# In one of the two depthwise pairs that need a second product, 128-row tiles give way to two rounds of 64x32 tiles, a VectorE tap, and a scan split three to one

## The chip, the cores and the metric

The kernel runs on one core of one Trainium2 chip. The metric is device microseconds from the start to the end of the program. The kernel before took 1713.65, 1717.79 and 1720.6 us in three runs (median 1717.79). One more execution was profiled; it took 1714.65 us, of which the trace spans 1712.9 us.

## The reference, cut to what matters

Four images of 128 channels and 96x96 points are group-normalised and read as sequences of 9216 points in four directions: along the rows, along the columns, and both backwards. Each of the 16 sequences goes through the same block, and the four directions are fused by a 1x1 convolution and added to the input.

```python
t = _grouped1x1(x, in_proj_w, in_proj_b, G)
u, gate = (t[:, :HID], t[:, HID:])
u = silu(u)
u = conv_general_dilated(u, dw_w, padding=[(2, 2)], feature_group_count=HID)   # depthwise, K = 5
s = conv1x1(u, ssm_in_w)
a = DMIN + (DMAX - DMIN) * sigmoid(conv1x1(u, ssm_delta_w, ssm_delta_b))
bb, cc = tanh(conv1x1(u, ssm_b_w, ssm_b_b)), tanh(conv1x1(u, ssm_c_w, ssm_c_b))
hst = exp(cumsum(log(a))) * cumsum(bb * s * exp(-cumsum(log(a))))
u = u + conv1x1(cc * hst + ssm_d * s, ssm_out_w)
u = _grouped1x1(u * sigmoid(gate), mix_w, mix_b, G)
return conv1x1(u, out_proj_w, out_proj_b)
```

The change concerns the five-tap depthwise convolution of the first 128 of the 256 hidden channels.

## The kernel before, in words

**Pairs and steps.** For each image the kernel makes a pass over columns (V) and one over rows (H); a pass treats a forward sequence and its backward partner together, as two streams s = 0 and 1. A pass has six stages of 16 lines. Within a stage the sequence is split by position modulo 4 into four phases p, each 384 points long. A *pair* is one phase of one stage for both streams; there are 192 pairs, numbered t. Four pairs make a *step* (48 steps), and k = t % 4 is the place in the step; the phases come in the order p = 1, 2, 3, 0. In the first three stages of a pass (`fresh`) the input projection is computed; in the last three the two streams meet stages that the other one has been through, and tiles are reused or read back mirrored.

**The convolution.** The hidden activations lie in a tile `sil` with 4 phases x 32 channels on 128 partitions, so that one product with a 128x32 matrix of diagonals (`band`, `conv`, L724) adds up to four taps of one phase. For p = 3 and p = 0 (`alone`, L733; k = 2 and 3) the 128-row product holds four taps, and the fifth is added by VectorE from an extra tile `lone` in `add_lone` (L768, L775), which also moves the sum from PSUM to the tile `u`. For p = 1 and p = 2 (k = 0 and 1) the taps fall three and two on either side of a block border: the 128-row product takes one side, and a 64-row product (`less`, `conv_less`, L784), of which eight tiles of 64x32 run side by side, takes the two taps of the other. ScalarE then copies the sum from PSUM banks 6 and 7 to `u` (`copy_u`, L801). The other 128 channels get their five taps from ScalarE (first tap, L826) and VectorE (L828) in PSUM banks 0 and 1.

**One pair.** All instruction streams are written in order by hand (`pair_on`, L1041). TensorE has, in each pair: the output products of the pair before the last six (`accumulate`, two of 8 matmuls, results in banks 2 or 4 and 5), the convolution, then gate or input projections and the products from the scan (`out_of`, L650, banks 0 to 3), then the projection of `u` (`proj`, 16 matmuls with the weights `main`, banks 4 and 5). In fp32 each matmul of the source is two instructions in the trace. ScalarE copies the output products out of PSUM into tiles `ys` (L946), which GpSimd adds to the accumulator `acc` (`add`, L963). VectorE multiplies by the gate (L711), runs the scan (L903: 64 partitions, two halves of 768 elements at k = 0 and k = 1), and makes the statistics of the next image. GpSimd makes the scan's operands (L876, L877) and its outputs (`outputs`, L909, L910, L912).

**What orders the adds.** `settle` (L1071) issues a pair's two GpSimd adds, or keeps them in the list `held`. In pairs with k = 3 both were held to the end of the pair. In three pairs, t = 55, 103 and 151 (`late`, L1041 on), the first results of a new image come up, and the accumulator is being reloaded by DMA; there both adds are held to the next pair, where they stand behind that pair's `outputs`. The tiles `ys` come from a ring of four.

Of the kernel before, what the change touches and what calls it, by code (L numbers as in the profile page):

```python
# [47 lines left out]
P = 128  # L48
# [21 lines left out]
def conv_preact_kernel(  # L70
# [58 lines left out]
    def mm(o, col, lhsT, rhs, start, stop):  # L129
        r = slice(32 * col, 32 * col + 32)  # L130
        nc.tensor.matmul(o[r, : rhs.shape[-1]], lhsT, rhs, start=start, stop=stop,  # L131
                         skip_group_check=True)


    gmeans = wp.tile([P, 2, P], F32, name="gmean")
    gmean = gmeans[:, 0, :]
# [12 lines left out]
    for e in range(2):  # L149
        nc.gpsimd.tensor_copy(gmeans[:, 1, bass.ts(e, 64)], gmeans[:, 0, bass.ts(1 - e, 64)])  # L150
# [17 lines left out]
    def stats_of(b):  # L168
        if b not in stats:
            stats[b] = sp.tile([P, NSC, 6], F32, tag="bn", name=f"bn_{b}")  # L170
        return stats[b]
# [5 lines left out]
    def stats_first(b):  # L177
# [15 lines left out]
        for e in range(2):  # L193
            product(pv[:, e : e + 1], gmeans[:, e, :], ex)
# [137 lines left out]
    rp = ctx.enter_context(tc.tile_pool(name="shared", bufs=1))  # L332

    def shared():
        return rp.tile([P, 16 * P], F32, tag="shared", name="shared")

# [3 lines left out]
    first_table = wp.tile([P, 1], F32, name="first_table")  # L340
# [4 lines left out]
    w_out_fuse = shared()  # L345
# [22 lines left out]

    def less_rows(s, p):
# [4 lines left out]
    less = wp.tile([P, R, 4, 32], F32, name="less")  # L374
    w_fin = wp.tile([P, 4, 2, P], F32, name="w_fin")
    b_fin = wp.tile([P, 1], F32, name="b_fin")
    id32 = wp.tile([P, 32], F32, name="id32")
# [5 lines left out]
    for s in range(2):  # L383
        for p in range(R):
            for k in range(2):
                r, to = slice(0, P), band[:, s, p]
                if k == less_of(p):
                    r, to = less_rows(s, p), less[:, p]
# [120 lines left out]
    def stage_of(step, f):  # L509
        return lone[step][:, 2 * (f % 2) : 2 * (f % 2) + 2, :]  # L510
# [222 lines left out]
    def alone(p):  # L733
        return p in (0, R - 1)
# [20 lines left out]
    def lone_tile(step):  # L755
        if step % NS in (0, 2) and step > 1:
            t = shared()[:, : 4 * (N + 1)]
        else:
            t = wk.tile([P, 4 * (N + 1)], F32, tag="lone", bufs=1, name=f"lone_{step}")
        return t.rearrange("p (a n) -> p a n", n=N + 1)  # L760

    def load_lone(step):
        lone[step] = lone_tile(step)
        nc.sync.dma_start(
            lone[step].rearrange("p (e s) n -> p e s n", e=2), edge_of(step).rearrange("e p s n -> p e s n")
        )

    def add_lone(i, banks):  # L768
        step, p = units[i]["step"], units[i]["p"]
        k = less_of(p)  # L770
        if fresh(step):
            slots = lone[step][:, 2:0:-1] if p else lone[step][:, 0::3]
        else:
            slots = lone[step][:, 3::-3] if p else lone[step][:, 1:3]
# [9 lines left out]
    def conv_less(i, banks, copy=True):  # L784
        step, p = units[i]["step"], units[i]["p"]
        sil, k, b0 = blocks(step), less_of(p), min(banks)
        for g in range(4):
            for s in range(2):
                r = less_rows(s, p)
                mm(bank(b0 + s), g, less[r, p, g, :], columns(step, sil[s][r, g, :], k),  # L790
                   False, True)
        if copy:
            copy_u(i, banks)

# [683 lines left out]
```

## Time and profile before

| what | before |
|---|---|
| three runs, us | 1713.65, 1717.79, 1720.6 |
| profiled execution, us (its span) | 1714.65 (1712.9) |
| TensorE matmul busy, us | 1691.0 (99%) |
| VectorE busy, us | 1505.1 (88%) |
| ScalarE busy, us | 1495.4 (87%) |
| GpSimd busy, us | 1481.7 (87%) |
| DMA moved | 350.79 MB, mean 205 GB/s |

Rows of a timeline give start and length in us, engine, source line, operation, written tile `<-` read tiles, shapes and how many instructions are merged; a bracket at the end says how long the engine sat idle before, and what ended that. A shape such as 128\*32 in a matmul's row is the tile of the array: rows by columns. The tiles of one round start some ns apart, so the start of the next group, not the length that is shown, tells what a group costs.

### The profile page before, as it was taken

The page shows a single profiled execution, that of the slowest core. Times are in us where ns is not written, and L with a number is a line of the kernel's source. Part 1 is how long each engine was busy: PE and PEld are TensorE (multiplying, and loading weights), DVE is VectorE, ACT ScalarE, POOL GpSimd, SP SyncE. Part 2 cuts the span into 40 slices and gives each one's busy share as a digit, 9 for nine tenths or more (in the row PEclk, how much of TensorE's full clock was granted, in tenths as well). Part 3 has the DMA queues.
Part 4 walks back from the last instruction along what each step waited for, and adds up shares of the span by engine and source line. Part 5 has one row for each costly group of instructions (what it writes and reads, how often), then busy time and mean ns, then how long its engine had stood idle before and what let it go on. Part 6 is the DMA issues. An engine that isn't in the chain of part 4 may idle for free.

```text
span 1712.9 us, 49914 instructions
## 1 busy us (share of the span) xinstructions
PE 1691.0 (99%) x20410; PEld 663.9 (39%) x20410; DVE 1505.1 (88%) x1506; ACT 1495.4 (87%) x2435; POOL 1481.7 (87%) x1455
## 2 busy tenths in 40 slices
PE   7999999999999999999999999999999999999998
PEld 3333333333333333333333333333333333333333
DVE  6899999888789999888888999988888888888897
ACT  4789999889889899888998898988998898988875
POOL 3689999888789999988888989999888889998887
PEclk9999999999999999999999999999999999999999
DMA  7855884468994788437897488633799538853365
GB/s 240 224 161 180 258 243 140 136 191 242 277 279 157 224 238 230 129 132 226 241 293 241 154 264 258 187 117 128 232 304 272 193 125 245 241 149 119 130 226 169
DMA packets 138949, 350.79 MB, mean 205 GB/s; under 512 B 18913, under 2 KB 85345, under 8 KB 138721
## 3 DMA queue, kind: packets, MB, share of 16 engines
q1 hardware_dynamic: 138576, 347.56, 66.7%
q8 instruction: 161, 2.64, 0.7%
q14 instruction: 68, 0.55, 0.1%
q10 hardware_dynamic: 144, 0.04, 0.0%
HBM read 191.46 MB, written 121.18 MB: 183 GB/s over the span
## 4 chain that ended last, share of the span: by engine, by line
PE 95%; DMA 3%; DVE 1%; ACT 1%; issue 0%; SPq 0%; DVEq 0%
PE psum L131 78%; PE psum L650 7%; PE psum L630 5%; PE psum L492 5%; DMA acc<-in_xr 1%; DMA sil<-sil 1%; DMA gate<-kept 1%; DVE u L711 0%; DVE bn L330 0%; DVE psum L828 0%; SPq L328 0%; PE psum L1289 0%; PE psum L1296 0%; DVE u L775 0%; PE psum L1304 0%
## 5 line engine op out<-in xcount | busy, mean ns | idle before, releaser
L828 DVE SCALAR_TENSOR_TENSOR psum<-sil,small,psum 128x768 f32<-128x768 f32 x576 | 589.1, 1023 | 52.7 <-ACT psum L826 33.8
L131 PE MATMUL psum<-u,w_fin 128*32 128x384 f32 (+1 forms) x6192 | 567.3, 485 | 3.4 <-DVE u L711 2.4
L131 PE MATMUL psum<-u,main 128*32 128x384 f32 x6144 | 535.2, 489 | 0.8 <-DVE u L775 0.4
L963 POOL TENSOR_TENSOR acc<-ys,acc 128x384 f32<-128x384 f32 x375 | 442.3, 1202 | 12.5 <-ACT ys L944 1.9
L711 DVE SCALAR_TENSOR_TENSOR u<-gate,psum 128x768 f32<-128x768 f32 x376 | 342.0, 951 | 121.1 <-PE psum L650 52.3
L131 PEld LDWEIGHTS psum<-u,w_fin 128*32 128x32 f32 x6192 | 191.2, 110 | 321.9 <-issue 233.3
L662 ACT COPY psum<-u 128x768 f32<-128x768 f32 x382 | 300.2, 798 | 12.0 <-DVE u L711 4.2
L131 PEld LDWEIGHTS psum<-u,main 128*32 128x32 f32 x6144 | 180.5, 110 | 329.3 <-issue 222.2
L131 PE MATMUL psum<-sil,band 128*32 128x384 f32 x3072 | 301.6, 488 | 0.5 <-ACT shared L516 0.5
L909 POOL TENSOR_TENSOR t<-t,t 64x384 f32<-64x384 f32 (+1 forms) x192 | 261.8, 1364 | 39.2 <-DVE t L903 22.4
L650 PE MATMUL psum<-t,main 32*128 32x384 f32 x1536 | 292.2, 521 | 0.6 <-ACT psum L662 0.5
L876 POOL TENSOR_SCALAR t<-tm 64x384 f32<-64x384 f32 x191 | 179.5, 940 | 107.7 <-ACT tm L865 95.4
L910 POOL TENSOR_TENSOR t<-t,t 64x384 f32<-64x384 f32 (+1 forms) x192 | 238.4, 1241 | 15.1
L877 POOL TENSOR_TENSOR t<-t,tm 64x384 f32<-64x384 f32 x192 | 237.5, 1237 | 15.3
L828 DVE SCALAR_TENSOR_TENSOR u<-sil,small,psum 128x768 f32<-128x768 f32 x192 | 194.9, 1015 | 6.8
L826 ACT ACTIVATE psum<-sil,small 128x768 f32<-128x768 f32 x191 | 171.7, 899 | 19.1 <-DVE u L711 16.5
L946 ACT COPY ys<-psum 128x384 f32<-128x384 f32 x288 | 137.9, 479 | 34.2 <-PE psum L131 27.7
L131 PEld LDWEIGHTS psum<-sil,band 128*32 128x32 f32 x3072 | 99.4, 110 | 150.8 <-issue 96.3
L630 PE MATMUL psum<-x_in,wn 32*128 32x384 f32 x768 | 154.2, 499 | 0.0
L492 PE MATMUL psum<-x_in,wn 32*128 32x385 f32 x704 | 143.8, 504 | 1.1 <-ACT shared L516 1.1
L650 PEld LDWEIGHTS psum<-t,main 32*128 32x128 f32 x1536 | 128.7, 184 | 33.8 <-issue 5.7
L505 ACT ACTIVATE sil<-psum,bnorm 128x385 f32<-128x385 f32 x176 | 102.1, 582 | 40.4 <-PE psum L650 20.0
(114 smaller groups left out, 1667.3 us busy)
## 6 DMA issues: line engine op xcount, KB each, us to landing
gate<-kept SPq DMA_DIRECT2D x106, 768.0 KB, 5.8
kept<-gate SPq DMA_DIRECT2D x82, 768.0 KB, 3.8
sil<-sil SPq DMA_DIRECT2D x32, 770.0 KB, 7.9
sil<-shared SPq DMA_DIRECT2D x240, 96.2 KB, 3.1
x_in<-in_xs SPq DMA_DIRECT2D x194, 96.2 KB, 3.3
out<-acc SPq DMA_DIRECT2D x46, 384.0 KB, 7.0
x_in<-in_xs SPq DMA_DIRECT2D x88, 192.5 KB, 5.8
acc<-in_xr SPq DMA_DIRECT2D x39, 384.0 KB, 6.4
```

The source lines that it names most:

```text
L131: nc.tensor.matmul(o[r, : rhs.shape[-1]], lhsT, rhs, start=start, stop=stop, skip_group_check=True)
L492: nc.tensor.matmul(bank(banks[2 * j + s])[:, : N + 1], stats[units[step * UB]["b"]][0][a, s, :], x_in[s][a, q, :], start=True, stop=True,)
L630: nc.tensor.matmul(bank(to)[:, :N], stats[un["b"]][0][r, s, :], x_in[s][r, q, off : off + N], start=True, stop=True)
L650: nc.tensor.matmul(bank(ssm(bi, s) + j)[:, :N], w_so[r, bass.ts(j, P)], z[r, :], start=(bi, s) not in seeded, stop=True, skip_group_check= ...
L662: nc.scalar.copy(psum[:, ssm(bi, s) : ssm(bi, s) + 2, :N], us[bi][:, s])
L711: nc.vector.scalar_tensor_tensor(v, g, 1.0, pz, ALU.add, ALU.mult)
L828: nc.vector.scalar_tensor_tensor(us[i][:, :, 1, :] if k == K - 1 else part, src, w_tap[:, k : k + 1], part, ALU.mult, ALU.add,)
L876: nc.gpsimd.tensor_scalar(*decay(i))
L877: nc.gpsimd.tensor_mul(ta[0:64, p, :], tb[0:64, :], tm[0:64, :])
L909: engine.tensor_mul(ta[0:64, p, r], tb[64:P, r], ta[64:P, p, r])
L910: engine.tensor_add(tb[0:64, r], ta[0:64, p, r], tb[0:64, r])
L963: adder.tensor_add(part, y, part)
```

## The change

In 37 of the 48 steps (not steps 0, 1 and 4, nor the last stage of a pass) one of the pairs with k = 0 and 1 is made `rich`: the one with p = 2 (k = 1) in fresh steps, with p = 1 (k = 0) in mirrored ones. There the convolution of four taps is done as two rounds of 64x32 tiles (`conv_half`), and the middle tap goes to VectorE's `add_lone`, so that `copy_u` falls away. Both rounds add into the same two PSUM banks, from opposite halves of the array's rows for each stream; between them stand the first output product on TensorE and, on ScalarE, a new two-element copy `turned` out of those banks, for which the second round waits. The scan is cut at a quarter or at three quarters, so that the shorter part falls into the rich pair. The stage tiles `lone` and `shared` grow from four to six rows and keep the middle phases too, the tile `less` shrinks to half, the statistics tile has one buffer in place of two, and the ring of `ys` has three tiles in place of four. In pairs with k = 3 the first add is now issued at once, and the second is held to the next pair.

```diff
+    def rich(un):
+
+        step, st, p = un["step"], un["st"], un["p"]
+        if step in (0, 1, 4) or st == NS - 1:
+            return False
+        return p == (2 if fresh(step) else 1)
...
+    def conv_half(i, banks, turn):
+
+        step, p = units[i]["step"], units[i]["p"]
+        sil, k, b0 = blocks(step), less_of(p), min(banks)
+        for g in range(4):
+            for s in range(2):
+                r = less_rows(1 - s if turn else s, p)
+                w = band[r, s, p, g, :] if turn else less[r, p - 1, g, :]
+                at = columns(step, sil[s][r, g, :], 1 - k if turn else k)
+                mm(bank(b0 + s), g, w, at, not turn, bool(turn))
...
-    def scan(step, part):
+    def scan(step, part, cut=N // 2):
...
-            scan(t // R - 1, k)
+            cut = N // 2
+            for e in range(2):
+                if rich(units[2 * (t - k + e)]):
+                    cut = N * (3 if e else 1) // 4
+            scan(t // R - 1, k, cut)
...
-            ys = wk.tile([P, N], F32, tag="ys", bufs=4, name=f"ys_{bu['id']}")
+            ys = wk.tile([P, N], F32, tag="ys", bufs=3, name=f"ys_{bu['id']}")
...
-        def settle(add):
+        def settle(add, wait=False):
             if add:
-                held.append(add) if late or k == R - 1 and not last else add()
-
-        ahead_of = not single and not last
+                held.append(add) if late or wait else add()
+
+        ahead_of = not single and not trio and not last
         first = add_next(2) if ahead_of else None
+        if trio:
+            conv_half(i, banks, 0)
+            nc.scalar.copy(turned, psum[:, banks[0] : banks[0] + 2, 0])
         if n:
             under(bi, 1)
+        if trio:
+            first = add_next(w[0])
...
-        conv(i, banks, single, (0,) if split else (0, 1))
+        if trio:
+            conv_half(i, banks, 1)
+        else:
+            conv(i, banks, single, (0,) if split else (0, 1))
...
-        if single:
+        if single or trio:
             add_lone(i, banks)
...
-        settle(add_next(w[1]))
+        settle(add_next(w[1]), k == R - 1 and not last)
...
-        if not late:
+        if last:
             for add in held:
                 add()
             held.clear()
```

What moves, at three places of pairs t = 56 and 57 (step 14, the third stage of the second image's V pass; t = 57 is rich). The names carry image order, stage, phase and stream: `u_2_2_2_0` is the pair t = 57, `u_2_2_1_0` the pair t = 56, `ys_2_0_1_0` an output product six pairs older.

TensorE from the projection of t = 56 to that of t = 57, before:

```order
L131 MATMUL psum_72<-u_2_2_1_0_5474,main_130 32x384 x16
L131 MATMUL psum_72<-u_2_0_3_0_4911,w_fin_144 32x384 x8
L131 MATMUL psum_72<-sil_14_5043,band_142 32x384 x8
L131 MATMUL psum_72<-sil_14_5043,less_143 32x384 x8
L131 MATMUL psum_72<-u_2_0_3_0_4911,w_fin_144 32x384 x8
L630 MATMUL psum_72<-x_in1_71,wn_1_2476 128x384
L650 MATMUL psum_72<-t1_2_0_0_0_5064,main_130 128x384 x4
```

The same place after (`band` is read here in its 64-row halves):

```order
L131 MATMUL psum_72<-u_2_2_1_0_5482,main_130 32x384 x16
L131 MATMUL psum_72<-sil_14_5051,less_143 32x384 x8
L131 MATMUL psum_72<-u_2_0_3_0_4918,w_fin_144 32x384 x8
L131 MATMUL psum_72<-sil_14_5051,band_142 32x384 x8
L131 MATMUL psum_72<-u_2_0_3_0_4918,w_fin_144 32x384 x8
L636 MATMUL psum_72<-x_in1_71,wn_1_2477 128x384
L656 MATMUL psum_72<-t1_2_0_0_0_5072,main_130 128x384 x4
```

The number of matmuls is the same; the convolution now stands first, in two pieces with an output product between them.

VectorE in the pairs t = 56 and 57, before:

```order
L828 SCALAR_TENSOR_TENSOR u_2_2_1_0_5474<-sil_14_5043,small_91,psum_72 128x2x384
L903 SCALAR_TENSOR_TENSOR t0_13_5161<-t0_13_5161,t0_12_4788 64x768
L711 SCALAR_TENSOR_TENSOR u_2_0_3_0_4911<-gate0_176,psum_72 128x768 x2
L828 SCALAR_TENSOR_TENSOR psum_72<-sil_14_5043,small_91,psum_72 128x2x384 x3
L828 SCALAR_TENSOR_TENSOR u_2_2_2_0_5570<-sil_14_5043,small_91,psum_72 128x2x384
L903 SCALAR_TENSOR_TENSOR t0_13_5161<-t0_13_5161 64x768
L711 SCALAR_TENSOR_TENSOR u_2_0_0_0_5001<-gate1_177,psum_72 128x768 x2
```

The same after:

```order
L849 SCALAR_TENSOR_TENSOR u_2_2_1_0_5482<-sil_14_5051,small_92,psum_72 128x2x384
L924 SCALAR_TENSOR_TENSOR t0_13_5168<-t0_13_5168,t0_12_4794 64x1152
L717 SCALAR_TENSOR_TENSOR u_2_0_3_0_4918<-gate0_171,psum_72 128x768 x2
L849 SCALAR_TENSOR_TENSOR psum_72<-sil_14_5051,small_92,psum_72 128x2x384 x3
L849 SCALAR_TENSOR_TENSOR u_2_2_2_0_5587<-sil_14_5051,small_92,psum_72 128x2x384
L785 SCALAR_TENSOR_TENSOR u_2_2_2_0_5587<-shared_5052,small_92,psum_72 128x2x384
L924 SCALAR_TENSOR_TENSOR t0_13_5168<-t0_13_5168 64x384
L717 SCALAR_TENSOR_TENSOR u_2_0_0_0_5008<-gate1_172,psum_72 128x768 x2
```

The scan (the rows that write `t0`) goes from 768 and 768 elements to 1152 and 384, and the fifth tap from `shared` stands ahead of the short part.

ScalarE in the pair t = 56, which follows a `late` pair, with the engines whose semaphores each row waits for, before:

```order
L946 COPY ys_2_0_2_0_5471<-psum_72 128x384 [waits DVE_49,PE_49]
L662 COPY psum_72<-u_2_0_3_0_4911 128x2x384 [waits Activation_49]
L662 COPY psum_72<-u_2_0_3_0_4911 128x2x384 [waits DVE_49]
L801 COPY u_2_2_1_0_5474<-psum_72 128x2x384 [waits PE_49]
L946 COPY ys_2_0_2_1_5514<-psum_72 128x384 [waits PE_49]
L666 ACTIVATE gate1_177<-psum_72,bnorm_1_2477 128x384 [waits DMAHW7_49,PE_49]
```

The same after:

```order
L967 COPY ys_2_0_2_0_5479<-psum_72 128x384 [waits DVE_49,PE_49]
L668 COPY psum_72<-u_2_0_3_0_4918 128x2x384 [waits Activation_49]
L668 COPY psum_72<-u_2_0_3_0_4918 128x2x384 [waits DVE_49]
L822 COPY u_2_2_1_0_5482<-psum_72 128x2x384 [waits PE_49]
L967 COPY ys_2_0_2_1_5522<-psum_72 128x384 [waits PE_49,Pool_49]
L672 ACTIVATE gate1_172<-psum_72,bnorm_1_2478 128x384 [waits DMAHW3_49,PE_49]
```

The rows stand as they stood; the copy of the pair's second output product has a wait for GpSimd that it did not have. With three tiles in the ring it takes the tile of `ys_2_0_1_0`, the first of the two held products, so it waits for that product's add.

More of the change, by code (lines that the diff above doesn't have):

```diff
@@ L339, in conv_preact_kernel @@
     nc.gpsimd.memset(mid, MID)
-    first_table = wp.tile([P, 1], F32, name="first_table")
+    turned = wp.tile([P, 2], F32, name="turned")
+    first_table = turned[:, 0:1]
     nc.gpsimd.memset(first_table, 1.0)
@@ L367, in less_of, with alone @@
         return 1 if p < 2 else 0
+    def alone(p):
+        return p in (0, R - 1)
     def less_rows(s, p):
@@ L789, in conv_less @@
                 r = less_rows(s, p)
-                mm(bank(b0 + s), g, less[r, p, g, :], columns(step, sil[s][r, g, :], k),
+                mm(bank(b0 + s), g, less[r, p - 1, g, :], columns(step, sil[s][r, g, :], k),
                    False, True)
@@ L808, in less_both @@
                 r = less_rows(s, p)
-                mm(bank(banks[s]), g, less[r, p, g, :], columns(step, sil[s][r, g, :], k), False, True)
+                mm(bank(banks[s]), g, less[r, p - 1, g, :], columns(step, sil[s][r, g, :], k), False, True)
     def new_u(i):
@@ L1045, in pair_on @@
         un = units[i]
-        single = alone(un["p"])
+        single, trio = alone(un["p"]), rich(un)
         step, g = divmod(t + R, R)
@@ L1103, in pair_on @@
         held.clear()
-        settle(first if ahead_of or split else add_next(w[0]))
-        if not single:
+        settle(first if ahead_of or split or trio else add_next(w[0]))
+        if not (single or trio):
             conv_less(i, banks, False)
```

56 lines of the change are left out of this document (28 added, 28 removed).

## The prediction

> **What bounds the kernel now.** I read the page's first table and its chain first, then TensorE's timeline over three pairs.
>
> ```profile
> PE 1691.0 (99%) x20410; PEld 663.9 (39%) x20410; DVE 1505.1 (88%) x1506; ACT 1495.4 (87%) x2435; POOL 1481.7 (87%) x1455
> PE 95%; DMA 3%; DVE 1%; ACT 1%; issue 0%; SPq 0%; DVEq 0%
> ```
>
> TensorE is busy 99% of the span and carries 95% of the chain; three more engines are at 87 to 88%. So a matmul less is time saved, and a stall of TensorE is time lost in full, while the others have about an eighth of the span in reserve, not everywhere. TensorE's timeline, columns start and length in us:
>
> ```profile
> 508.68 1.48 PE L131 MATMUL psum<-sil,band 128*32 128x384 f32 x16
> 510.08 0.88 PE L131 MATMUL psum<-sil,less 64*32 64x384 f32 x16
> 510.89 1.50 PE L131 MATMUL psum<-u,w_fin 128*32 128x384 f32 x16
> ...
> 513.08 0.50 PE L630 MATMUL psum<-x_in,wn 32*128 32x384 f32 x3
> ...
> 513.90 2.79 PE L131 MATMUL psum<-u,main 128*32 128x384 f32 x32
> ...
> 523.01 2.79 PE L131 MATMUL psum<-u,main 128*32 128x384 f32 x32
> 525.62 0.83 PE L131 MATMUL psum<-sil,band 128*32 128x384 f32 x8
> 526.26 1.47 PE L131 MATMUL psum<-u,w_fin 128*32 128x384 f32 x16
> 527.55 0.83 PE L131 MATMUL psum<-sil,band 128*32 128x384 f32 x8
> 528.20 1.47 PE L131 MATMUL psum<-u,w_fin 128*32 128x384 f32 x16
> ...
> 531.18 1.18 PE L131 MATMUL psum<-u,main 128*32 128x384 f32 x12
> ```
>
> No row has a bracket: TensorE runs through. From projection to projection a pair with a `less` product takes 523.01 - 513.90 = 9.11 us, one without it 531.18 - 523.01 = 8.17. So one 64-row round costs 0.94, changes of tile shape included.
>
> **Part 1: the matmuls, -13.0 us.** The two `band` rows take 526.26 - 525.62 = 0.64 and 528.20 - 527.55 = 0.65: together 1.29 for a 128-row convolution. Before, a rich pair pays 1.29 + 0.94; after, two 64-row rounds, each between 128-row work as now, 2 x 0.94. It saves 1.29 - 0.94 = 0.35 us. There are 37 such pairs: 13.0 us. That is the whole gain; nothing else leaves TensorE.
>
> **Part 2: VectorE's tap and the scan, 0 in most pairs.** VectorE's rows for t = 56 and 57, and the tap's group:
>
> ```profile
> 510.53 2.14 DVE L903 TENSOR_TENSOR_SCAN t<-t,t 64x768 f32<-64x768 f32 x1
> 513.42 1.82 DVE L711 SCALAR_TENSOR_TENSOR u<-gate,psum 128x768 f32<-128x768 f32 x2 [0.75 <-PE psum L650]
> ...
> 519.64 1.84 DVE L903 TENSOR_TENSOR_SCAN t<-t 64x768 f32<-64x768 f32 x1
> 522.53 1.82 DVE L711 SCALAR_TENSOR_TENSOR u<-gate,psum 128x768 f32<-128x768 f32 x2 [1.05 <-PE psum L650]
> ```
>
> ```profile
> L775 DVE SCALAR_TENSOR_TENSOR u<-shared,small,psum 128x768 f32<-128x768 f32 x46 | 46.4, 1008 | 0.0
> ```
>
> A scan of 768 elements takes 1.84 where nothing holds it, 2.4 ns an element, so the long part is 0.92 longer and the short one 0.92 shorter. In the rich pair +1.01 for the tap and -0.92 for the scan cancel. In the other pair VectorE idles 0.75 to 1.05 between scan and gate, and that idle time is the cover for 0.92; where it is 0.17 short the delay falls on a pair that has slack. If the cover were gone altogether, 37 x 0.92 would be 34 us, but VectorE waits here for TensorE. The ScalarE copy that goes (0.8 us) waits for TensorE as well and frees nothing that is waited for.
>
> In three pairs (t = 37, 85, 133) there is no such cover, because the weights of the next image are scaled there:
>
> ```profile
> 342.09 2.12 DVE L903 TENSOR_TENSOR_SCAN t<-t 64x768 f32<-64x768 f32 x1
> 344.32 0.78 DVE L259 TENSOR_SCALAR wn<-main,inv 128x128 f32<-128x128 f32 x1
> 345.02 1.80 DVE L711 SCALAR_TENSOR_TENSOR u<-gate,psum 128x768 f32<-128x768 f32 x2
> ```
>
> The gate multiplication follows at once, without idle time. The longer scan delays it by up to 0.92, and the pair behind has no 64-row round to lend time. Between 0 and 2.8 us for the three; I take half, +1.5.
>
> **Part 3: the ring of three, +11.7 us.** In t = 56, 104 and 152, behind the late pairs, the second output product's copy takes the `ys` tile of a held product, and that product's add stands behind the pair's scan outputs on GpSimd. GpSimd's rows, and ScalarE's copy:
>
> ```profile
> 509.83 1.22 POOL L909 TENSOR_TENSOR t<-t,t 64x384 f32<-64x384 f32 x1
> 511.14 2.50 POOL L910 TENSOR_TENSOR t<-t,t 64x384 f32<-64x384 f32 x1
> 513.71 0.50 POOL L912 COPY t<-t 64x384 f32<-64x384 f32 x1
> 514.28 3.59 POOL L963 TENSOR_TENSOR acc<-ys,acc 128x384 f32<-128x384 f32 x3
> ```
>
> ```profile
> 512.46 0.48 ACT L946 COPY ys<-psum 128x384 f32<-128x384 f32 x1 [0.30 <-PE psum L131]
> ```
>
> The first of the adds ends at 514.28 + 1.20 = 515.48, 2.5 us behind the end of the copy (512.46 + 0.48), which today does not wait for it. Moreover L910 takes 2.50 beside the 1.22 of its twin L909, because it ends with VectorE's scan (510.53 + 2.14 = 512.67); t = 56 gets the long scan part, so L910 and the add move another 0.92, to 516.40. The copy then ends at 516.9. Behind it on ScalarE queue the two gate activations, the first tap for VectorE, and the release of banks 6 and 7; and TensorE's last gate product, which starts at 513.08, needs the copy's bank 5. It starts at about 517.0: a stall of 3.9 us, of which nothing comes back on a bound engine. At the least, without the scan's 0.92, it is 3.0. Three times 3.9 is 11.7. In ordinary steps the same wait finds its add done: the first add of k = 3 is now issued at once, a pair earlier.
>
> **Part 4: the clock, +5.1 us.** The trace shows once what such a stall does. TensorE's rows around 470 us, and the windows there (the columns behind the engines' busy times are the granted clock, the DMA share and GB/s):
>
> ```profile
> 465.89 2.79 PE L131 MATMUL psum<-u,main 128*32 128x384 f32 x32
> 471.03 1.84 PE L131 MATMUL psum<-u,w_fin 128*32 128x384 f32 x16 [2.35 <-DVE u L711]
> ...
> 479.21 1.18 PE L131 MATMUL psum<-u,main 128*32 128x384 f32 x12
> ```
>
> ```profile
> 472.00:474.00 2.00, 2.00 (x20) 0.88 (x16) 1.93 (x3) 1.92 (x5) 1.49 (x2) 0.51 1.08 245
> 474.00:476.00 2.00, 2.00 (x28) 0.32 (x20) 1.93 (x3) 1.97 (x3) 2.00 (x3) 0.63 1.06 367
> ```
>
> TensorE idled 2.35 us, and then ran at a granted clock of 0.51 and 0.63: 2 x 0.49 + 2 x 0.37 = 1.7 us lost. The whole pair took 479.21 - 465.89 = 13.32 in place of 9.11. A stall of 3.9 us leaves TensorE about 3.3 us without a matmul, more than the 2.35. I charge 1.7 to each of the three: 5.1, with 0 as the lower bound.
>
> [...]
>
> **Part 5: the added wait `turned`, 0.** The second 64-row round waits for ScalarE's copy of two elements, which stands behind the previous pair's scaling L886. What queues behind that copy are the copies for the scan's products, whose products TensorE wants later in the pair.
>
> ```profile
> 526.96 0.62 ACT L886 ACTIVATE t<-t,small 64x384 f32<-64x384 f32 x1
> ```
>
> ```profile
> L520 ACT ACTIVATE shared<-mid 128x1 f32<-128x1 f32 x28 | 5.7, 203 | 0.9
> L868 ACT COPY t<-psum 64x384 f32<-64x384 f32 x192 | 90.1, 469 | 9.1 <-PE psum L131 1.7
> ```
>
> L886 ends at 527.58, 1.96 us after the pair's start at 525.62. TensorE wants the second round after 0.94 + 1.29 = 2.23. The nearest row for the copy is L520, one element in 0.20: ready at 2.16. The other bound is L868, a copy of 384 elements out of PSUM in 0.47: ready at 2.43, 0.2 late. I take L520's, for the size, and so no cost; the upper end is 37 x 0.2 = 7.4 us.
>
> The rest goes together at nothing: the split DMA of the stage tile, the smaller `less`, and the single statistics buffer stand far from a use.
>
> **The sum.** -13.0 + 1.5 + 11.7 + 5.1 = +5.3 us on the profiled execution's 1714.65, so 1720.0. The median of the three runs lies 3.1 above that execution; on it the sum would be 1723.1. I predict the middle, 1721.5. A difference of 0.5%, 8.6 us, is about what a measurement of this kernel can tell from none, so this forecast is no change: a gain that is eaten by three stalls.
>
> **Rivals.**
>
> *The clock stays full* (1714.9). [...] Against it: 2.35 us were enough once. 20%.
>
> *The handshake costs* (slower, 1727.4). The copy `turned` takes nearer 0.47 than 0.20, or starts late because the gate multiplication ahead of it was late; each rich pair stalls by 0.2 at its second round, 7.4 us more, +12.7 in all. It decides from 0.09 us a pair on, since (8.6 - 5.3) / 37 = 0.09. For it: the slack by rows is only 0.07. Against it: L886's end is tied to TensorE's own projection, and a two-element copy is much nearer to L520. 17%.
>
> *The late copy is hidden* (faster, 1703.2). The three stalls do not show, because GpSimd gets its add done in time: -13.0 + 1.5 = -11.5. For it: nothing in the trace, unless the adds came before the outputs; against it: the wait stands in the order, and the add ended 2.5 us too late even before. 8%.
>
> **How the numbers follow.** The forecast keeps 55%. The low end, 1709, is the forecast with stalls of 3.0 us and no loss of clock (-13.0 + 9.0 = -4.0), on the fastest of the three runs (1713.65 - 4.0 = 1709.7); the high end, 1730, is the handshake rival on the median's footing (1730.5). Outside lie the hidden copy and the ends of the handshake. Faster by over 0.5% is the hidden copy and 2% for what I overlooked, 10%; slower is the handshake and 5% for smaller stalls on top of the forecast, 22%; 68% is left for no change.
>
> **What would show it.** TensorE's rich pairs take 8.76 us between projections where they took 9.11; if they take 8.9 and more, part 5 failed. In t = 56, 104 and 152 TensorE's last gate product starts some 4 us late with ScalarE's `ys` as the releaser, and the `ys` copy itself shows idle time that GpSimd's add ended; without that, part 3 is wrong and the time is near 1703. Behind each of them windows of 2 us should show a granted clock near 0.5. GpSimd's busy time should not change, VectorE's should rise by some 37 us.

## The result, and the profile after

The changed kernel took 1729.29 us (median of six runs, 1724.96 to 1736.43); the kernel before, in the same comparison, 1715.35 us. The ratio is 1.008, with a 95% interval of 1.0062 to 1.0098: about 14 us slower, and clear of the 0.5% named in the prediction. The profiled execution took 1730.94 us, 16.3 more than that of before; the spans of the two traces, 1729.1 and 1712.9 us, lie 16.2 apart.

The page's first table of the changed kernel:

```profile
PE 1691.4 (98%) x20410; PEld 651.2 (38%) x20410; DVE 1525.7 (88%) x1543; ACT 1469.8 (85%) x2435; POOL 1449.3 (84%) x1451
```

TensorE's busy time has not fallen (1691.0 before). Both the saving and the half clock are in this sum, since a matmul at half clock is recorded as longer: in the projection of t = 57 most take 847 ns, where 486 is the median of one at full clock (windows 516.02:519.43 and 526.02:528.70). So the place of the time has to be found pair by pair, from one projection to the next. TensorE around t = 56 and 57, and further on the projections of t = 59 and t = 60:

```profile
511.29 0.49 PE L636 MATMUL psum<-x_in,wn 32*128 32x384 f32 x2
514.73 0.91 PE L636 MATMUL psum<-x_in,wn 32*128 32x384 f32 x2 [2.96 <-ACT ys L967]
515.57 4.48 PE L131 MATMUL psum<-u,main 128*32 128x384 f32 x32
519.98 0.88 PE L131 MATMUL psum<-sil,less 64*32 64x384 f32 x16
520.78 1.50 PE L131 MATMUL psum<-u,w_fin 128*32 128x384 f32 x16
522.21 0.88 PE L131 MATMUL psum<-sil,band 64*32 64x384 f32 x16
523.02 1.50 PE L131 MATMUL psum<-u,w_fin 128*32 128x384 f32 x16
...
526.02 2.79 PE L131 MATMUL psum<-u,main 128*32 128x384 f32 x32
...
542.36 2.79 PE L131 MATMUL psum<-u,main 128*32 128x384 f32 x32
...
551.12 1.18 PE L131 MATMUL psum<-u,main 128*32 128x384 f32 x12
```

The rich pair t = 60 takes 551.12 - 542.36 = 8.76 us, as worked out (9.11 before). The rich pair t = 57 takes 526.02 - 515.57 = 10.45: its projection, 2.79 otherwise, takes 4.48. And ahead of it stands the predicted wait, with the predicted releaser. GpSimd's and ScalarE's rows there:

```profile
507.75 1.22 POOL L930 TENSOR_TENSOR t<-t,t 64x384 f32<-64x384 f32 x1
509.05 3.31 POOL L931 TENSOR_TENSOR t<-t,t 64x384 f32<-64x384 f32 x1
512.42 0.50 POOL L933 COPY t<-t 64x384 f32<-64x384 f32 x1
513.00 4.61 POOL L984 TENSOR_TENSOR acc<-ys,acc 128x384 f32<-128x384 f32 x4
```

```profile
514.20 0.48 ACT L967 COPY ys<-psum 128x384 f32<-128x384 f32 x1 [4.16 <-POOL acc L984]
```

L931 takes 3.31 us (2.50 before); it ends with the scan, whose part here is longer. The first of the four adds ends at 513.00 + 4.61 / 4 = 514.15, ScalarE's copy starts at 514.20 after 4.16 us without work, and TensorE gets bank 5 at 514.73. The granted clock behind it (third column from the end):

```profile
514.00:516.00 2.00, 1.27 (x10) 0.53 (x14) 0.00 (x0) 1.29 (x3) 2.00 (x3) 1.00 0.00 0
516.00:518.00 2.00, 2.00 (x20) 0.70 (x16) 0.92 (x1) 1.87 (x3) 1.61 (x2) 0.50 0.32 79
518.00:520.00 2.00, 2.00 (x20) 0.46 (x12) 1.93 (x3) 0.58 (x1) 0.91 (x1) 0.64 0.74 303
```

2 x 0.50 + 2 x 0.36 = 1.7 us are lost. What TensorE waited for shows the same three times, and something else. From the list of the kernel before, and then of the changed one, these are the longest rows but for the load at the start of the program, which is in both (total, times, longest):

```profile
PE psum L131 <- DVE u L711: 2.4, 1, 2.4
PE psum L492 <- ACT shared L516: 1.1, 1, 1.1
```

```profile
PE psum L636 <- ACT ys L967: 8.8, 3, 3.0
PE psum L131 <- DVE u L717: 4.9, 3, 1.8
PE psum L131 <- ACT lone L522: 2.2, 2, 1.6
PE psum L131 <- ACT gate L678: 1.2, 3, 0.4
```

The first row after is the ring. The second and third lie in t = 50 to 52, 100, 146 and 148, and no step of the prediction has them. VectorE and SP show where the second comes from, here for t = 52, in the changed kernel and then in the kernel before:

```profile
468.10 1.82 DVE L717 SCALAR_TENSOR_TENSOR u<-gate,psum 128x768 f32<-128x768 f32 x2 [4.05 <-DMA gate<-kept]
```

```profile
454.44 3.96 SPq L529 DMA_DIRECT2D sil<-lone  x4
458.65 0.38 SPq L693 DMA_DIRECT2D gate<-kept  x1
```

```profile
469.16 1.82 DVE L711 SCALAR_TENSOR_TENSOR u<-gate,psum 128x768 f32<-128x768 f32 x2 [4.83 <-DMA gate<-kept]
```

VectorE's gate multiplication waits for a kept gate read back by DMA. In the changed kernel this load is issued at 458.65, behind four seam DMAs of the stage tile (`sil<-lone`, `new_stage`), which hold SP's queue for 3.96 us, and by the trace it lands at 467.97, 9.3 us after its issue. The third row is the same thing a step further on: at t = 50 and 146 ScalarE's `lone` comes late behind a gate multiplication that waited for its load (1.35 and 2.45 us on VectorE). The kernel before has the same wait once, 2.4 us on TensorE at t = 52; it stands in the prediction's fences, where only the clock behind it was read.

With the times from projection to projection in both traces, the 16.2 us between the spans fall into these parts:

| part | predicted | measured |
|---|---|---|
| 37 rich pairs | -13.0 | -10.8 |
| t = 37 to 39, 85 to 87, 133 to 135 (weights scaled) | +1.5 | +1.0 |
| t = 56, 104, 152 (ring): 3.8, 4.5, 3.8 | +11.7 | +12.1 |
| t = 57, 105, 153 over 8.76 (clock): 1.7, 2.1, 1.7 | +5.1 | +5.5 |
| the other pairs of t = 43 to 54, 91 to 102, 139 to 150 | 0 | +6.6 |
| the rest, and both ends of the program | 0 | +1.8 |
| sum | +5.3 | +16.2 |

### The profile page after: what moved, and what is told of

Same layout as the page of the kernel before. It is cut to its first block, busy times and chain, and to the rows that moved or that the text cites. A ratio compares the mean times of both kernels' runs of the same rounds, so it can differ in the third digit from the quotient of the medians.

```text
span 1729.1 us, 50173 instructions
## 1 busy us (share of the span) xinstructions
PE 1691.4 (98%) x20410; PEld 651.2 (38%) x20410; DVE 1525.7 (88%) x1543; ACT 1469.8 (85%) x2435; POOL 1449.3 (84%) x1451
## 3 DMA queue, kind: packets, MB, share of 16 engines
q1 hardware_dynamic: 148720, 347.56, 66.9%
## 5 line engine op out<-in xcount | busy, mean ns | idle before, releaser
L984 POOL TENSOR_TENSOR acc<-ys,acc 128x384 f32<-128x384 f32 x375 | 411.0, 1119 | 17.0 <-ACT ys L965 3.2
L930 POOL TENSOR_TENSOR t<-t,t 64x384 f32<-64x384 f32 (+1 forms) x192 | 232.2, 1209 | 104.6 <-PE psum L656 67.5
L131 PEld LDWEIGHTS psum<-u,w_fin 128*32 128x32 f32 x6192 | 186.3, 109 | 335.7 <-issue 231.8
L931 POOL TENSOR_TENSOR t<-t,t 64x384 f32<-64x384 f32 (+1 forms) x192 | 292.9, 1526 | 15.0
L131 PE MATMUL psum<-sil,band 128*32 128x384 f32 (+1 forms) x3072 | 278.2, 488 | 2.8 <-ACT lone L522 2.2
L898 POOL TENSOR_TENSOR t<-t,tm 64x384 f32<-64x384 f32 x192 | 202.9, 1057 | 17.9 <-ACT t L889 2.8
L636 PE MATMUL psum<-x_in,wn 32*128 32x384 f32 x768 | 161.0, 505 | 8.8 <-ACT ys L967 8.8
L498 PE MATMUL psum<-x_in,wn 32*128 32x385 f32 x704 | 147.7, 507 | 1.1 <-ACT shared L522 1.1
L131 PEld LDWEIGHTS psum<-sil,band 128*32 128x32 f32 (+1 forms) x3072 | 86.0, 108 | 148.5 <-issue 73.9
```

The costliest lines, as they stand in the source:

```text
L131: return nc.tensor.matmul(o[r, : rhs.shape[-1]], lhsT, rhs, start=start, stop=stop, skip_group_check=True)
L498: nc.tensor.matmul(bank(banks[2 * j + s])[:, : N + 1], stats[units[step * UB]["b"]][0][a, s, :], x_in[s][a, q, :], start=True, stop=True,)
L636: nc.tensor.matmul(bank(to)[:, :N], stats[un["b"]][0][r, s, :], x_in[s][r, q, off : off + N], start=True, stop=True)
L898: nc.gpsimd.tensor_mul(ta[0:64, p, :], tb[0:64, :], tm[0:64, :])
L930: engine.tensor_mul(ta[0:64, p, r], tb[64:P, r], ta[64:P, p, r])
L931: engine.tensor_add(tb[0:64, r], ta[0:64, p, r], tb[0:64, r])
```

## The experiments

Ratios are to the kernel before, measured beside each run, with 95% intervals; kernel 2 is the kernel of experiment 2, and so on. "That stretch" is t = 43 to 54 with its repetitions 48 and 96 pairs later. The packets' times, added up over the 16 DMA engines, fill 0.91 to 0.95 of it in the kernel before, and 0.97 to 1.06 of each 10 us of its middle (430 to 490 us in the first repetition).

**1. The ring alone, in the kernel before.**

```diff
-            ys = wk.tile([P, N], F32, tag="ys", bufs=4, name=f"ys_{bu['id']}")
+            ys = wk.tile([P, N], F32, tag="ys", bufs=3, name=f"ys_{bu['id']}")
```

> The kernel before with a ring of three ys tiles and nothing else changed (the scan stays even, no rich pair). Ring theory: in t = 56, 104 and 152 ScalarE's copy of the second output product now ends its idle time with GpSimd's add, and TensorE's last gate product waits. The scan is 0.9 shorter there than in the changed kernel, so TensorE's wait is 2.96 - 0.9 = about 2.1 us instead of 2.96, and the three pairs get 2.9 longer instead of 3.8. With the clock at half behind it 1.7 more each: 3 x (2.9 + 1.7) = +13.8 us, ratio 1.008; if a wait of 2.1 leaves the clock alone, +8.7, ratio 1.005. Rival, DMA: the changed kernel is slower because its DMAs are cut into more packets in the stretch around t = 44 to 54, and the ring costs only what the three waits show beside it; then this kernel should gain nothing visible, +0 to +3 us, ratio under 1.002.

Measured: 1729.90 us, ratio 1.009 (1.0065 to 1.0115). TensorE's row in t = 56, ScalarE's copy, and the windows:

```profile
521.10 1.42 PE L630 MATMUL psum<-x_in,wn 32*128 32x384 f32 x2 [2.13 <-ACT ys L946]
```

```profile
520.57 0.48 ACT L946 COPY ys<-psum 128x384 f32<-128x384 f32 x1 [3.34 <-POOL acc L963]
```

```profile
521.00:523.00 2.00, 1.90 (x6) 0.49 (x10) 0.00 (x0) 0.97 (x3) 2.00 (x3) 0.59 0.04 8
523.00:525.00 2.00, 2.00 (x16) 0.59 (x12) 1.02 (x1) 1.76 (x3) 0.98 (x1) 0.50 0.41 94
525.00:527.00 2.00, 2.00 (x20) 0.66 (x16) 1.94 (x2) 0.58 (x1) 0.91 (x1) 0.50 0.74 300
527.00:529.00 2.00, 2.00 (x24) 0.69 (x20) 1.93 (x3) 1.08 (x3) 0.58 (x1) 0.70 0.27 102
```

One buffer less costs as much as the whole change: three waits of 2.13 to 2.15 us, after two of which the clock fell to 0.50, by the windows for 3.4 us behind the wait that ended at 944.32 and for 6.8 us behind the one that ended at 521.10. The ring theory holds; the rival, that this costs next to nothing, falls.

**2. The held adds first.** In the changed kernel:

```diff
             add_lone(i, banks)
+        if n > 2 and (n - 2) % (NP * 2) == 0:
+            for add in held:
+                add()
+            held.clear()
         recurrence(t)
```

> The changed kernel with the two held adds put ahead of GpSimd's scan outputs in t = 56, 104 and 152 only. Ring theory: ScalarE's copy finds its add done, TensorE's three waits (8.8 us in all) and the half clock behind them go: 3 x (3.8 + 1.7) = -16.5 us against the changed kernel, about 1713, ratio to before 0.998. Rival, the wait moves on: the scan outputs, now behind two adds and behind the long scan part, end some 2.5 us later and the next pair's products from the scan wait for them; then at least half of it stays, ratio 1.003 or more. Rival, DMA packets: only the waits go and the clock's part was something else, -9 us, ratio 1.003.

Measured: 1717.41 us, ratio 1.0013 (0.9998 to 1.0027): 1.008 - 1.0013 = 0.67%, 11.5 us less than the changed kernel, not 16.5. The waits shrank from 2.96 to 0.8 us each, and no half clock followed (1.00 in all windows from 513.50 to 527.50 us); but t = 56 still takes 10.74. GpSimd's row says why:

```profile
512.27 3.87 POOL L984 TENSOR_TENSOR acc<-ys,acc 128x384 f32<-128x384 f32 x2 [1.65 <-DMA acc<-in_xr]
```

The adds now wait for the reload of `acc`, which is why they had been held. The rest of the shortfall shows in that stretch, where this profiled execution waited 8.4 us in all for the gates, more than any other. It took 1724.04 us, 6.6 above the kernel's median, so its trace shows more of this than the median has.

**3. The scan cut evenly.** In the changed kernel:

```diff
-            cut = N // 2
-            for e in range(2):
-                if rich(units[2 * (t - k + e)]):
-                    cut = N * (3 if e else 1) // 4
-            scan(t // R - 1, k, cut)
+            scan(t // R - 1, k, N // 2)
```

> The changed kernel with the scan cut in the middle everywhere. By the prediction's steps: in t = 56, 104 and 152 the scan part is 0.92 shorter, so GpSimd's outputs and the add come 0.9 earlier, and each of the three waits falls from 2.96 to about 2.1: -2.8 us, with the clock perhaps up to -5 more. In the 37 rich pairs VectorE has the tap (1.01 us) on top of a full half scan: where the idle time ahead of the gate multiplication is 0.75 to 1.05, the gate multiplication comes 0 to 0.25 us late, 0 to 9 us in all. So -3 to +6 us against the changed kernel. Rival: the uneven scan is needed, because the tap and the scan also hold GpSimd; then rich pairs take 9.0 us and more and the sum is over +9.

Measured: 1736.02 us, ratio 1.0115 (1.0095 to 1.0136), 6 us slower than the changed kernel. The three waits are 2.16 us, 0.8 shorter, as expected; but the clock fell to 0.50 all the same. Rich pairs keep 8.76; the pair behind a rich one pays 0.46 in fresh steps, 0.3 to 0.7 in mirrored ones. The projections of t = 57 and 58:

```profile
528.57 2.79 PE L131 MATMUL psum<-u,main 128*32 128x384 f32 x32
537.20 2.79 PE L131 MATMUL psum<-u,main 128*32 128x384 f32 x32
```

537.20 - 528.57 = 8.63 in place of 8.17. So the split of the scan earns its place, and where the delay lands is the pair behind, not the rich one; I had put it at 0 to 0.25.

**4. The gate loads ahead of the seam DMAs,** in kernel 2:

```diff
+        load_kept(n + 2)
         if ahead is not None:
             new_stage(ahead, spots)
-        load_kept(n + 2)
```

> As the run with the adds first, and the load of the kept gates issued ahead of the stage tile's DMAs on SP's queue (in t = 51 SP issues the gate load at 463.96, behind four seam DMAs of 4.1 us, and it lands at 468.10, where VectorE has waited 4.05 for it). DMA-order theory: the waits of TensorE for the gate multiplication in t = 52, 100 and 148 (1.6, 1.8, 1.5 us in the changed kernel; 2.4, 0, 0 in the kernel before) go, and with them about 2 us a time: -6 us against the run with the adds first, ratio to before about 0.994. Rival, bandwidth: the 16 DMA engines are busy 98% in the stretch from t = 43 to 54, so what is issued earlier only makes something else late, and the time is the same within 2 us.

Measured: 1713.67 us, ratio 0.9990 (0.9977 to 1.0003), about 4 us less than kernel 2. No wait of TensorE for a gate is left in its trace. SP and VectorE, for t = 52:

```profile
454.51 0.81 SPq L693 DMA_DIRECT2D gate<-kept  x1
455.41 3.05 SPq L529 DMA_DIRECT2D sil<-lone  x4
```

```profile
464.71 1.82 DVE L717 SCALAR_TENSOR_TENSOR u<-gate,psum 128x768 f32<-128x768 f32 x2 [1.04 <-PE psum L656]
```

The load that is waited for is issued at 454.51, ahead of the seam DMAs, and lands at 463.30; VectorE waits for TensorE again, not for a DMA. (The expectation names the load issued at 463.96 in the changed kernel. That one lands at 472.81; the one waited for was issued at 458.65.) The order of issue matters, in this kernel.

**5. The same, in the kernel before.**

> The kernel before with the load of the kept gates issued ahead of the stage tile's DMAs, and nothing else. DMA-order theory: the wait of 2.4 us of VectorE's gate product in t = 52 and the half clock behind it go (13.3 us back to about 10), and in executions where t = 100 or 148 wait too, those as well: -2 to -4 us against the kernel before, ratio 0.998. Rival, bandwidth: the stretch is as full as before and only another load is late, ratio 1.000 within 0.001.

Measured: 1715.73 us, ratio 1.0003 (0.9991 to 1.0015). No gain: the wait of 2.4 us is gone from the trace, and the timed runs don't show it. That at TensorE's old pace the gates are in time but for now and then would explain it, but no count over the timed runs shows that.

**6. Four `ys` tiles, in the changed kernel.**

```diff
-            if (b, c) not in loaded and len(chunks) < 3:
+            if (b, c) not in loaded and len(chunks) < 2:
...
-                chunks[b, c] = wk.tile([P, SC], F32, tag="xs", bufs=3, name=f"xs_{b}_{c}")
+                chunks[b, c] = wk.tile([P, SC], F32, tag="xs", bufs=2, name=f"xs_{b}_{c}")
...
-            ys = wk.tile([P, N], F32, tag="ys", bufs=3, name=f"ys_{bu['id']}")
+            ys = wk.tile([P, N], F32, tag="ys", bufs=4, name=f"ys_{bu['id']}")
```

> The changed kernel with four ys tiles, as before; the room comes from the chunks of the statistics, two buffers in place of three (and at most two loaded ahead). Ring theory: ScalarE's copy in t = 56, 104 and 152 waits for no add, the waits of 8.8 us and the half clock behind them go in full, where the adds put first left 0.8 us of wait and 1.6 us of time in each: -16.5 us against the changed kernel, 1713, ratio to before 0.9985, and the three pairs take 9.11 again. Rival: statistics chunks loaded later hold SP's queue and with it gate loads, so that something of the 16.5 comes back in t = 43 to 54: ratio 1.003.

Measured: 1710.13 us, ratio 0.9975 (0.9962 to 0.9987), 1.05% or 18 us less than the changed kernel. The projections of t = 55, 56 and 57:

```profile
504.70 2.79 PE L131 MATMUL psum<-u,main 128*32 128x384 f32 x32
513.81 2.79 PE L131 MATMUL psum<-u,main 128*32 128x384 f32 x32
522.57 2.79 PE L131 MATMUL psum<-u,main 128*32 128x384 f32 x32
```

9.11 and 8.76: the ring's cost is gone whole. What remains in the trace are the waits for gates in that stretch:

```profile
471.30 1.78 PE L131 MATMUL psum<-u,w_fin 128*32 128x384 f32 x16 [3.86 <-DVE u L717]
```

```profile
469.42 1.82 DVE L717 SCALAR_TENSOR_TENSOR u<-gate,psum 128x768 f32<-128x768 f32 x2 [6.23 <-DMA gate<-kept]
```

**7. No pair rich, with everything else of kernel 2.** `rich` returns False.

> The run with the adds first, but no pair is rich: convolutions, copies and the even scan as in the kernel before, with the tiles, rings and DMAs of the changed kernel. It shows what the 37 pairs are worth by themselves, against the run with the adds first (1717.4). Theory of the sum: each rich pair saves 0.35, of which those in and near the stretch bound by DMA (t = 43 to 54, three pairs an image) and the three at t = 33, 81 and 129 bring nothing: 37 - 9 = 28 pairs, so 28 x 0.35 = +9.8 here, minus up to 3 for the scan of t = 56 and the weights' scaling at t = 37: 1724 to 1727, ratio to before 1.005 to 1.007. Rival, the pairs' saving is real only in the profile of TensorE and other waits take it back: 1717 to 1719, ratio 1.002 or less.

Measured: 1723.71 us, ratio 1.0055 (1.0038 to 1.0071). Against kernel 2 the 37 pairs are worth 1.0055 - 1.0013 = 0.42%, 7 us, give or take 0.2%, of the 13.0 that they save on TensorE. Kernel 4, which has the rich pairs and the early gate loads, lies 1.0055 - 0.9990 = 0.65% or 11 us below this one, while the early loads alone brought nothing in kernel 5: nearly the whole gain of the pairs comes through once the gates are early. Kernel 7 has the packets of the changed kernel (148720 on the main queue, 138576 before, for the same 347.56 MB) and in its one trace that stretch is as short as before's (below), which speaks against the smaller packets as what makes the gates late.

**8. Kernel 6 with the gate loads of 4.**

> Four ys tiles and the gate loads ahead of the stage tile's DMAs together, in the changed kernel. If both effects are as measured apart (gate loads 1717.4 to 1713.7, the ring's remaining 3 x 1.6): 1713.7 - 4.9 = about 1709, ratio 0.996, faster than both kernels. Rival: statistics with two buffers cost what the ring gives: 1714, ratio 0.999.

Measured: 1708.27 us, ratio 0.9965 (0.9949 to 0.9981). Faster than both kernels, by 6 us against before. Against kernel 6 the 0.1% lies within the intervals. TensorE no longer waits for a gate in the trace, but once, in t = 100, for a seam DMA that now stands behind the gate loads, and the clock falls to 0.50 there:

```profile
PE psum L131 <- DMA sil<-lone: 2.3, 1, 2.3
```

So in part the early load makes something else late, as the rival of experiment 4 had it.

**9. Kernel 6 without the rich pairs ahead of and in that stretch.**

```diff
-        if step in (0, 1, 4) or st == NS - 1:
+        if step in (0, 1, 4) or st == NS - 1 or 8 < step and step % 12 in (0, 1, 9, 10):
```

> The run with four ys tiles, without the 14 rich pairs of the steps ahead of and in the stretch where the DMAs are busy 98% (t = 36, 40, 49, 53, 84, 88, 97, 101, 132, 136, 145, 149, and 180, 184 in the last image, which has no such stretch behind it). DMA theory: what TensorE gains in these pairs it waits out in t = 52, 100 and 148 for gates that come no earlier; only the last two pairs bring their 0.35 each: +0.7 us and not over +1.5 against that run, 1711 to 1712, ratio to before 0.998. Rival: the gains land and the late gates are chance: 14 x 0.35 = +4.9, 1715, ratio 1.0005.

Measured: 1712.83 us, ratio 0.9991 (0.9978 to 1.0005): 0.16% or 2.7 us above kernel 6, in the middle between the 0.7 of the one theory and the 4.9 of the other, and the intervals reach both. Not decided.

**10. Kernel 6 without the stores of three images.**

```diff
-            nc.sync.dma_start(planes(out[b], at), planes(accf, at))
+            if b + 1 == B:
+                nc.sync.dma_start(planes(out[b], at), planes(accf, at))
```

> The run with four ys tiles, and the results of the first three images are not stored (some 9.4 us of 384 KB stores an image fall into the stretch from t = 43 to 56, about a sixth of its 22 MB). Bandwidth theory: the gates of t = 52, 100 and 148 then land in time; TensorE's waits there (3.9 us in the first, with the half clock behind it, then 1.5 and 1 in the run with four tiles, 4.4 us over the kernel before in all) go: -4 to -8 us against that run, 1702 to 1706. Rival: SP's own issue order, not the 16 engines, makes them late: SP loses only the issue time of the stores (about 0.5 us each) and the time stays within 2 us of 1710.

Measured: 1706.52 us, ratio 0.9955 (0.9940 to 0.9971), 0.2% or 3.4 us less than kernel 6, whose interval it still touches; the kernel leaves out three of the four results. The waits for gates fell from 6.3 us in three times to 1.2 in two in the traces. Less traffic goes with earlier gates, but brings less than the 4 to 8 us expected, and the stores also leave SP's queue. Order of issue (kernel 4 against 2) counts by the timed runs; for the traffic the traces speak, and the time only just.

**11. Kernel 8 with the output products earlier in the rich pairs.**

```diff
-        first = add_next(2) if ahead_of else None
+        first = add_next(2) if ahead_of or trio else None
...
-        if trio:
-            first = add_next(w[0])
+        second = add_next(w[1]) if trio else None
...
-        settle(add_next(w[1]), k == R - 1 and not last)
+        settle(second if trio else add_next(w[1]), k == R - 1 and not last)
```

> Four ys tiles and the early gate loads (1708.3), and in the rich pairs both output products stand 1.3 us earlier: one ahead of the first 64-row round, one between the rounds. Bank theory: in t = 33, 81, 129 (9.27 to 9.37 us in place of 8.77) and t = 53, 101, 149 (9.07) the first round waits for ScalarE's reading of banks 6 and 7; with a product ahead of it the six pairs come to 8.77 to 8.9: -2 us. Against it: the convolution ends 1.3 us later, so VectorE's tap, the scan and the gate multiplication start later in the 37 pairs, where they had about 1 us of idle time: 0 to +0.3 us a pair, up to +11. I expect 1706 to 1712; over 1712 the order of the change (convolution first) is what hides VectorE's tap.

Measured: 1739.48 us, ratio 1.0145 (1.0124 to 1.0167), 31 us above kernel 8. VectorE in the rich pair t = 57:

```profile
523.58 1.01 DVE L785 SCALAR_TENSOR_TENSOR u<-shared,small,psum 128x768 f32<-128x768 f32 x1 [1.51 <-PE psum L131]
524.63 1.01 DVE L924 TENSOR_TENSOR_SCAN t<-t 64x384 f32<-64x384 f32 x1
525.67 1.82 DVE L717 SCALAR_TENSOR_TENSOR u<-gate,psum 128x768 f32<-128x768 f32 x2
```

The tap waits 1.51 us for the convolution, and the gate multiplication follows at once. The rich pair t = 57 takes 9.21 (8.76 in kernel 4), and the one behind it 8.67 (8.17). Over all 37, against kernel 8, the rich pairs lose 16 us and the pairs behind them 17. The convolution at the head of the pair is what hides the tap, and the change's order is needed. Whether the banks would have been free in t = 33 and 53 can't be read from this kernel, since the delay lies over it.

The sum of the times of the 36 pairs of that stretch, from projection to projection, in one profiled execution of each kernel:

| kernel | us |
|---|---|
| before; 1; 5; 7; 9 (no rich pair there) | 318.1; 319.0; 316.8; 316.8; 318.3 |
| changed; 2; 6 (two rich pairs an image there) | 323.3; 328.2; 322.4 |
| 4; 8 (rich, gate loads first) | 314.8; 317.7 |
| 10 (kernel 6 without stores) | 314.9 |
| 3; 11 (rich, but with VectorE's delays) | 319.0; 319.0 |

The six rich pairs there should make it 6 x 0.35 = 2.1 us shorter. Where VectorE doesn't slow TensorE down, it became 4 to 10 us longer; with the gate loads first it is 0.4 to 3.3 us shorter. One execution each is thin evidence: that of kernel 2 took 6.6 us more than the kernel's median, that of kernel 4 3.2 us less.

## Why the prediction was right or wrong, by its steps

The forecast of 1721.5 us lies 7.8 below the measured median, which is inside the range but near its end. As a difference to the kernel before, +5.3 us were forecast and +13.9 came between the medians. The forecast called no change the likeliest, at 68%, and gave 22% to what came, slower by over 0.5%. That the range reached up to 1730 is owed to a rival that the runs refute (below), so it caught the time by luck.

**The matmuls (part 1)** were right per pair: 8.76 us. The sum of 13.0 came to 10.8. The 2.2 us that are missing are nearly all in six pairs: t = 33, 81 and 129 take 9.16 to 9.26, and t = 53, 101 and 149 take 9.08 where 8.85 was due. TensorE's row for t = 33:

```profile
304.00 0.88 PE L131 MATMUL psum<-sil,less 64*32 64x384 f32 x16 [0.34 <-ACT gate L678]
```

The first 64-row round needs banks 6 and 7 at once, where an output product stood in between before, and ScalarE is still reading them. I counted this move at nothing, because in most pairs nothing is late. With the even scan of kernel 3 the three pairs take 8.87 to 8.90, so most of this delay comes with the long scan part in the pair ahead. The other three take 8.86 in kernels 3, 4 and 8, where banks 6 and 7 are used in the same order, so the order alone doesn't explain them; what does stays open.

**The tap and the scan (part 2)** were right: no loss in most pairs, 1.0 us for t = 37, 85 and 133 where 1.5 was taken. Kernel 3 shows the price without the split, in the pair behind.

**The ring (part 3)** was right in mechanism, place, releaser and size: a stall of 3.9 was worked out and the three pairs grew by 3.8, 4.5 and 3.8. In the 4.5 some 0.7 us are the clock's, which fell there at 935.86, before the wait was over at 936.82. Kernels 1 and 6 show that the ring by itself makes and unmakes 14 to 18 us.

**The clock (part 4)** was right: 5.1 predicted, 5.5 measured; the rival in which the clock stays full falls, since the granted clock was 0.50 behind each of the three gaps. The gap of 2.35 us in the kernel before was no exception: over all the traces nine of ten gaps of 2.01 to 2.35 us were followed by 0.50. The three gaps themselves were 2.92 to 2.96 us, not the 3.3 worked out.

**The wait `turned` (part 5)** costs nothing, as forecast. The copy takes even less than the 0.20 taken for it:

```profile
L1104 ACT COPY turned<-psum x37: 160/161/162, 98.9 to 1633.3; 128x2 f32<-128x2 f32 x37
```

In t = 57 the second round starts 522.21 - 519.98 = 2.23 us behind the first, as worked out, without idle time. The rival that put 0.2 us on each rich pair gave 1727.4, close to the time measured, and is wrong: it had the sum by the wrong cause.

**The signs named at the end** came for the pairs, the releaser and the clock, but not for the busy times. VectorE's rose by 20.6 us, not 37: the taps' rows brought the 37, and the scan's took some 16 less. GpSimd's fell by 32.4 where no change was forecast. Why these operations got shorter was not looked into.

**What failed** is a term that the sum does not have. The prediction takes it that "a matmul less is time saved" and counts the rest "at nothing"; it has no term for the waits that a faster TensorE meets. The row with the bracket of 2.35 us at 471.03 stood in the prediction as evidence on the clock. Its releaser, VectorE's gate multiplication, was not followed to the DMA behind it, though the chain that ended last, in the kernel before, names this load with its 9.19 us:

```profile
459.84 9.19 DMA gate<-kept
```

Nor did I ask what becomes of it when the pairs around it get shorter. In the middle of that stretch the DMA engines were full before (0.97 to 1.06 by the packets' times), and TensorE's gain there turned into waits, five in place of one (1.6 and 0.6 us in t = 52 and 50, 1.8 in t = 100, 1.6 and 1.5 in t = 146 and 148): +6.6 us in the profiled execution. That the order of issue makes the gates late is shown by kernel 4 against 2 and 7; that the traffic does is supported by the traces of kernels 8 and 10, not settled by their times; how much of the gain of the 14 pairs ahead of the stretch is lost with it stays open after kernel 9.

## What to carry to other kernels

A buffer taken from a ring to make room is a term of its own: look for the one place where its tiles live longest, because there the new wait is paid in full (here 2.92 to 2.96 us three times), and a stall of 2 us and more was nearly always paid again here in the clock behind it (it fell to 0.50 behind 15 of the 16 gaps of 2.01 us and more). A gain on the bounding engine is only a gain where nothing else is full: take every wait that this engine shows already, follow it to its source, and ask whether it grows by what the engine gains. And a time that comes out near a forecast is no evidence for the cause; only the releaser of the wait is.

## What the runs showed of the hardware

**The clock and the length of a gap.** Of TensorE's gaps in these traces, the load at the start of the program apart, twelve lasted 1.3 to 2.0 us; behind eleven of them (1.98 the longest, in kernel 3) the granted clock stayed at 1.00 in all windows, behind one of 1.49, at 74 us in kernel 7, it fell to 0.50. Of ten between 2.01 and 2.35 (one in the kernel before, four in kernel 1, three in 3, one each in 5 and 8) nine were followed by 0.50, and one of 2.13, in kernel 1, was not, beside another of 2.13 in the same kernel that was. All six of 2.92 and more were (three in the changed kernel, two in 2, one in 6).

The trace of the changed kernel records a granted clock of 0.50 for 3.413 us from 516.02 and from 1362.52, and for 6.827 us from 935.86; that of the kernel before for 3.413 us from 472.05. So a fall cost 1.7 or up to 3.4 us, with no relation to the length of the gap that these few cases show: gaps of 2.35, 2.92 and 2.96 us went with 3.413, one of 2.95 with 6.827.

The three falls of the changed kernel lie 419.84 and 426.66 us apart, 123.0 and 125.0 times the recorded 3.413. In the last 3.41 us ahead of each TensorE was idle for 2.12, 1.99 and 2.06 us, in the kernel before for 2.35. That is read from these two traces alone; no run was made for it, and why one gap of 2.13 us in kernel 1 was followed by 0.50 and another was not stays open.

**Some TensorE products took longer where the ring was smaller.** With three `ys` tiles (the changed kernel) 25 pairs of the stages with wider input products take 0.06 us longer than with four (the kernel before), most of them 8.258 in place of 8.198: 1.5 us in all. The products that read `x_in` with 385 columns get longer there, 507 ns each in place of 504 in the mean; it is 507 in kernel 1 too, which has three tiles, and 504 in kernel 6, which has four:

```profile
L498 PE MATMUL psum<-x_in,wn 32*128 32x385 f32 x704 | 147.7, 507 | 1.1 <-ACT shared L522 1.1
```

```profile
L498 PE MATMUL psum<-x_in,wn 32*128 32x385 f32 x704 | 144.2, 504 | 1.1 <-ACT shared L522 1.1
```

The first row is of the changed kernel, the second of kernel 6. No run shows why.
